# Expert jobs of a DiT block: gathered rows turned by VectorE and dealt out by SyncE instead of turned by TensorE, in eight of sixteen jobs

## The chip, the cores and the metric

The kernel runs on one core of one Trainium2 chip. The metric is the device time of one execution in microseconds, as the median of three runs. The profiler was on for one further execution, and its trace is what all rows below come from. TensorE is called PE, VectorE DVE, ScalarE ACT, GpSimd POOL and SyncE SP, as in the profile.

## The reference, cut to what matters

A transformer block with attention and a mixture of experts, where each expert chooses its tokens. There are 16 x 256 = 4096 tokens of 256 features and 8 experts, so an expert takes 512 tokens.

```python
x = x + o @ Wout.T                            # after attention
tok = x.reshape(-1, d)
gate = jax.nn.softmax(tok @ Wgate.T, axis=-1)
vals, idx = jax.lax.top_k(gate.T, k_cap)      # each expert's 512 tokens
g = _ln(tok[idx_flat], mlp_g, mlp_b).reshape(k_cap, E, d)
y = jnp.einsum('ked,ehd->keh', g, fc1s) + b1s
y = jax.nn.gelu(y, approximate=True)
y = jnp.einsum('keh,edh->ked', y, fc2s) + b2s
y = y * w[..., None]
tok = tok.at[idx_flat].add(y.reshape(-1, d))
```

## The kernel before, in words

Attention comes first, sequence by sequence, in an order written out by hand (the list PLACES). It stores each token's normalised row, without gain and bias, in a DRAM tensor `xn_dram`, and the token itself in the output. The experts follow in 16 jobs of 256 tokens: jobs 0 to 7 are the first halves of the eight experts' lists, jobs 8 to 15 the second halves. Jobs 0 and 1 run inside the ordered plan. For the others there is a loop over `k` from 2 to 15 (L1889) with one iteration a job, and that loop is all that the change touches.

An iteration runs job `k` (`a`) and prepares job `k + 1` (`new`) and job `k + 2` (`far`). It goes through 16 steps `s`, or 15 in iterations 7 to 14 (`seven`). Each engine executes its instructions in the order in which the steps issue them, and SP and POOL issue their DMAs in that order too. What a job needs, with the step before the change:

- `rows` (L1361) for `far`, at step 2, on DVE: which places of the list this job fills. Every second job also needs its pair's counts and sums (`lay_out`, L1874).
- `list_matmul` (L1370) and `take` (L1381) for `new`, at steps 3 and 4 (5 and 6 in iteration 7): PE makes the list in the one PSUM buffer of `pls`, and DVE takes the token numbers into `idx`. `take_gates` (L1392), `gather` (L1398) and `gather_gates` (L1405) come a step later: on POOL two indirect DMAs bring 2 x 128 rows of `xn_dram` into `xg`, and two more the gates into `few`.
- `transposes` (L1414) and `evict` (L1435) for `new`, at step 14 (13 in iterations of 15 steps): PE turns the rows, four 128x128 transposes into `px`, and ACT writes them to `xT` with gain and bias, two activations of 128x256.
- `up` (L1447) and `gelu` (L1455) for job `k`, at steps 0 to 7: one of eight chunks of the hidden layer each.
- Second layer of job `k`, steps 8 to 15. In iterations 2 to 6 and 15 `down` takes a fourth of a half at each step, and `finish` (L1545) writes the weighted rows `y` at steps 11 and 15. In iterations 7 to 14 seven products of half-size blocks take the place of eight (the table SEVEN, L1850): DVE makes sums of weights (`sum_w`, L1477, steps 3 to 6) and of hidden values (`sum_h`, L1486, steps 7 to 10), PE the products (`seventh`, L1495, steps 8 to 14), and DVE adds them up (`mix`, `begin`, `complete`, steps 9 to 14 and step 0 of the next iteration). The first product that reads a sum of hidden values is number 6, at step 9.
- `scatter` (L1551) of job `k - 1` at steps 8 and 12, on POOL: two indirect DMAs that add `y` to the output.
- `far.load()` (L1357) at the end of the iteration, on SP: the 1 MB of w2, the bias row, the 1 MB of w1. They go to the two buffers that the jobs use in turn, so w2 is issued when PE has read job `k`'s w2 for the last time.

In iterations 2 to 6 the second routing runs alongside (`second_routing`, L1865): every fifth step PE counts (`count_three`, L1159, into `pc`), DVE chooses two bits, sets three candidates and compares (`choose_bits` L1163, `compare_three` L1150). The counts fall on steps 4, 9 and 14 of iteration 3, and 3, 8 and 13 of iteration 4. A count reads what the compare before it made.

DVE's transpose turns blocks of 32x32. Attention already uses it with `exchange` (L610): four DMAs on SP, each of which takes 32 partitions apart and lays them out over 128.

Of the kernel before, what the change touches and what calls it, by code (L numbers as in the profile page):

```python
# [9 lines left out]
F32 = mybir.dt.float32  # L10
I32 = mybir.dt.int32
BF16 = mybir.dt.bfloat16
AF = mybir.ActivationFunctionType
# [5 lines left out]
P = 128  # L19
B, N, D = 16, 256, 256  # L20
H, HD = 16, 64
E, DD = 8, 1024
# [5 lines left out]
DC = D // P  # L28
HP = H // 2
FC = DD // P  # L30
KC = CAP // P
KL = KC // 2
CAPL = CAP // 2
SQ = 32
QB = P // SQ
# [3 lines left out]
LN1_G, LN1_B, B_ADA, MLP_G, MLP_B = 0, 2, 4, 6, 8  # L39
# [4 lines left out]
class Plan:  # L44
# [7 lines left out]
    def step(self, place, engine, took, run, needs=(), makes=(), tiles=(), mode=0, lag=0.1):  # L52
        k = len(self.steps)
        self.steps.append((place, engine, took, run, needs, tiles, mode, lag))
        for m in makes:
            self.makers.setdefault(m, []).append(k)
# [7 lines left out]
def kernel(  # L64
# [14 lines left out]
    nc = tc.nc  # L79
# [7 lines left out]
    few = const.tile([P, NVEC + DC * (B + E)], F32, name="few")  # L87
    nc.scalar.dma_start(few, small)
    vec = few[:, :NVEC]
# [133 lines left out]
    PRB = 6  # L223
# [263 lines left out]
    if True:  # L487
        attw = ctx.enter_context(tc.tile_pool(name="attw", bufs=1))
        seq = ctx.enter_context(tc.tile_pool(name="seq", bufs=2))
        work = ctx.enter_context(tc.tile_pool(name="work", bufs=2))  # L490
        stat = ctx.enter_context(tc.tile_pool(name="stat", bufs=4))
        moe = ctx.enter_context(tc.tile_pool(name="moe", bufs=2))
# [114 lines left out]
            engine.tensor_scalar(ws, ws, -1.0 / HD, 1.0, ALU.mult, ALU.mult)  # L607
            engine.tensor_tensor(w3, w3, by_head(ws), ALU.add)

        def exchange(dst, src):  # L610

            for k in (0, 2, 1, 3):
                nc.sync.dma_start(dst[:, k, :], src[k * SQ : (k + 1) * SQ])

        def by_head(x):
            return x.unsqueeze(1).unsqueeze(3).to_broadcast([P, QB, 8, HD // QB])
# [32 lines left out]
        class First:  # L649
# [48 lines left out]
            def evict_too(self, c):  # L698
                b = self.b
                nc.vector.tensor_scalar(  # L700
                    self.out()[:, c, :], self.pt[c], vec[:, LN1_G + c : LN1_G + c + 1],
                    bias1[:, c, b : b + 1], ALU.mult, ALU.add,
                )
# [12 lines left out]
        class Group:  # L716
# [80 lines left out]
            def turn(self, kb):  # L797
                if self.t == 0:
                    kb.append(work.tile([P, QB, TB, HP // 2, SQ], F32, tag="pb", bufs=3, name="kb"))
                nc.vector.transpose(  # L800
                    kb[0][:, :, self.t],
                    self.qk.rearrange("p (q h d) -> p q h d", q=QB, d=SQ),
                )
# [11 lines left out]
            def affine(self):  # L815
                if self.g < 2:
                    qT = of_sequence(qTs, self.b, "qT", [P, HP, N])
                    for t in range(TB):
                        nc.scalar.activation(
                            qT[:, 4 * self.g : 4 * self.g + 4, bass.ts(t, P)].rearrange(  # L820
                                "p h (k m) -> p k h m", m=SQ
                            ),
                            self.raw[:, :, t], AF.Identity, bias=qgb[:, 1:2], scale=qgb[:, 0:1],
                        )
                    return
                kT = self.raw.rearrange("p k t h m -> p (k t h m)")
                nc.scalar.activation(  # L827
                    kT, kT, AF.Identity,
                    bias=vec[:, KN_B : KN_B + 1], scale=vec[:, KN_G : KN_G + 1],
                )  # L830
# [510 lines left out]
        class Job:  # L1341
# [28 lines left out]
            def list_matmul(self):  # L1370
                self.pls = ps.tile([P, KL, P + 2], F32, tag="po", name="pls")
                self.xg = seq.tile([P, KL, D], F32, tag="xs", bufs=5, name="xg")
                self.at = moe.tile([P, KL], F32, tag="at", bufs=4, name="at")
                self.idx = moe.tile([P, 2, KL], I32, tag="idx", bufs=4, name="idx")
                for c in range(KL):
                    nc.tensor.matmul(
                        self.pls[:, c], self.row[:, 1, bass.ts(c, P)], self.pair.ranked,
                        start=True, stop=True,
                    )
# [23 lines left out]
                    )  # L1403

            def gather_gates(self):  # L1405
                self.few = moe.tile([P, KL, E], F32, tag="w", bufs=4, name="few")
                for c in range(KL):
                    nc.gpsimd.indirect_dma_start(
                        out=self.few[:, c, :], out_offset=None, in_=gate_drams[self.tiles][:, :],
                        in_offset=bass.IndirectOffsetOnAxis(ap=self.idx[:, 1, c : c + 1], axis=0),  # L1410
                    )
                self.w = self.few[:, :, self.e]
# [10 lines left out]
            def turned(self):  # L1423
                if self.xT is None:
                    self.xT = seq.tile([P, DC, CAPL], F32, tag="hT", name="xT")
                return self.xT

            def evict_too(self, i):
                c, part = DC - 1, bass.ts(i, P)
                nc.vector.tensor_scalar(  # L1430
                    self.turned()[:, c, part], self.px[c][:, part], vec[:, MLP_G + c : MLP_G + c + 1],
                    vec[:, MLP_B + c : MLP_B + c + 1], ALU.mult, ALU.add,
                )

            def evict(self, chunks=DC, part=slice(0, CAPL)):  # L1435
                for c in range(chunks):
                    nc.scalar.activation(  # L1437
                        self.turned()[:, c, part], self.px[c][:, part], AF.Identity,
                        bias=vec[:, MLP_B + c : MLP_B + c + 1],
                        scale=vec[:, MLP_G + c : MLP_G + c + 1],  # L1440
                    )
                if part.stop == CAPL:
                    self.hid = seq.tile([P, FC, CAPL], F32, tag="qT", name="hid")
                    self.y = work.tile([P, KL, D], F32, tag="pr", bufs=PRB, name="y")
                    self.ph, self.py = {}, {}

            def up(self, f):  # L1447
                self.ph[f] = ps.tile([P, CAPL], F32, tag="sc", bufs=4, name="ph")
# [124 lines left out]
        at = plan.step  # L1573
# [29 lines left out]
        for b in range(B):  # L1603
# [56 lines left out]
            for d in range(HP // 2):  # L1660
                a = Quad(b, d)
                p = base + d * QUAD
# [3 lines left out]
                for i in range(2):  # L1666
                    q = p + 3 * i
                    m = n + (i,)
                    sums, pb, prT = ("sums",) + m, ("pb",) + m, ("prT",) + m
                    scs = [("sc",) + m + (j,) for j in range(2)]  # L1670
                    at(q, "PE", 0.84, partial(a.scores, i), [("qT", b, g), ("kT", b, g)], [("sc",) + m], scs + [("qT", b), ("kT", b)], mode=1, lag=0.22)
                    for j in range(2):
                        nmax, pr, pp = ("nmax",) + m + (j,), ("pr",) + m + (j,), ("sc", 1) + m + (j,)
# [172 lines left out]
        for k in plan.order(PLACES):  # L1846
            plan.steps[k][3]()

        LIST_AT, TURN_AT = 5, 14
        SEVEN = {  # L1850
            3: [("sum_w", 0)], 4: [("sum_w", 1)], 6: [("sum_w", 2), ("sum_w", 3)], 7: [("sum_h", 2)],
            8: [("seventh", 0), ("sum_h", 0)],
# [28 lines left out]
        def listed(job, waits):  # L1881
            yield from ([],) * waits
            yield from ([job.list_matmul], [partial(job.take, c) for c in range(KL)])
            yield [job.take_gates, job.gather, job.gather_gates]
# [4 lines left out]
        for k in range(2, len(jobs)):  # L1889
            a = jobs[k]  # L1890
            new = jobs[k + 1] if k + 1 < len(jobs) else None
            far = jobs[k + 2] if k + 2 < len(jobs) else None
            ahead = k + 1 if k + 1 in FRESH else k + 2
            parts = lay_out(jobs[ahead]) if ahead < len(jobs) and k + 2 not in FRESH else iter(())
            lists = listed(new, 5 if k + 1 in FRESH else 3) if new else iter(())
            more = lay_out(far) if k + 1 in FRESH and far else iter(())
            seven = k in SEVENTHS
            SCATTER_AT = (8, 12) if new else (2, 6)
            if seven:
                a.c = {}  # L1900
            for s in range(15 if seven else 16):
                if k - 1 in SEVENTHS and s == 0:
                    for name, *args in SEVEN[15]:
                        getattr(jobs[k - 1], name)(*args)
                if seven:
                    for name, *args in SEVEN.get(s, ()):
                        getattr(a, name)(*args)
                for step in next(rest, ()):
                    step()
                for step in next(parts, ()):  # L1910
                    step()
                for step in next(lists, ()):
                    step()
                if s > LIST_AT + 4:
                    for step in next(more, ()):
                        step()
                if s in SCATTER_AT:
                    jobs[k - 1].scatter(SCATTER_AT.index(s))
                if new and s == TURN_AT - seven:
                    new.transposes()  # L1920
                    new.evict()
                if s < FC:
                    a.up(s)
                    a.gelu(s)
                    if s == FC - 1:
                        a.weigh()
                elif not seven:
                    i, q = divmod(s - FC, 4)
                    a.down(i, 2 * q, 2 * q + 2)
                    if q == 3:  # L1930
                        a.finish(i)
                        if not new:
                            a.scatter(i)
            if far:
                far.load()
# [54 lines left out]
```

## Time and profile before

| what | us |
|---|---|
| median of 3 runs | 982.57 |
| lowest and highest run | 981.4, 983.54 |
| the profiled execution, its own time | 981.85 |
| its span | 980.1 |
| PE busy | 965.4 |
| DVE busy | 790.2 |
| POOL busy | 654.9 |
| ACT busy | 593.7 |

The span is the time from the first to the last instruction. Busy time counts an engine's own instructions. A line such as L1419 is the line of the kernel that issued an instruction. `out<-in` names tiles. A timeline row gives start, duration, engine, line, operation and count, and in brackets how long the engine had been idle and what ended that. "us to landing" is from the issue of a DMA to its end. The loop begins at about 771 us, and its iterations 3, 4, 9, 10 and 11 begin, with their first `up`, at 786.02, 800.84, 873.59, 887.51 and 901.33.

### The profile page before, as it was taken

What the parts mean: (1) busy time and instruction counts of PE and PEld (TensorE: products, weight loads), DVE (VectorE), ACT (ScalarE), POOL (GpSimd) and SP (SyncE); (2) the same over time, 40 slices, a digit from 0 to 9 for tenths busy, and PEclk for the clock granted to TensorE, in tenths of its full rate; (3) what the DMA queues carried; (4) which work ended last, traced back from release to release, by engine and by line L of the source; (5) the groups of instructions that cost most, each with busy time, mean ns of one, the idle gap of its engine ahead of it and who ended that gap; (6) DMA issues with size and microseconds to landing.
All of it is one profiled execution on the core that took longest, in us unless ns stands there. A gap on an engine that the chain in (4) does not pass through costs nothing.

```text
span 980.1 us, 22623 instructions
## 1 busy us (share of the span) xinstructions
PE 965.4 (99%) x7628; PEld 567.7 (58%) x7628; DVE 790.2 (81%) x1919; ACT 593.7 (61%) x1684; POOL 654.9 (67%) x1069
## 2 busy tenths in 40 slices
PE   9999999999999999999999999999999999999996
PEld 5544544444454545444444544545557888899995
DVE  6678988898899999888899899989975465677661
ACT  2788676667666677667667677666784332343441
POOL 4687677767797886776777677777536435555663
PEclk9999999999999999999999999999999999999998
DMA  8013666666677676667566666777663666776672
GB/s 282 2 43 96 165 176 154 160 168 162 162 189 182 169 173 173 163 174 171 147 175 175 161 168 166 174 178 177 172 189 108 211 183 166 213 200 186 189 221 30
DMA packets 153666, 160.54 MB, mean 164 GB/s; under 512 B 16080, under 2 KB 146640, under 8 KB 153552
## 3 DMA queue, kind: packets, MB, share of 16 engines
q1 hardware_dynamic: 143968, 147.50, 56.5%
q0 software_dynamic: 7168, 8.53, 4.9%
q10 hardware_dynamic: 2416, 3.08, 1.0%
q8 instruction: 61, 1.00, 0.4%
q14 instruction: 53, 0.43, 0.1%
HBM read 53.94 MB, written 12.84 MB: 68 GB/s over the span
## 4 chain that ended last, share of the span: by engine, by line
PE 89%; DMA 3%; issue 2%; DVE 2%; ACT 1%; POOL 1%; SPq 1%; POOLq 0%; DVEq 0%; ACTq 0%
PE pm L519 33%; PE sc L853 12%; PE pw L519 11%; PE po L939 11%; PE ph L1450 10%; PE seven L1506 5%; PE py L1466 4%; DMA out<-y,idx 1%; PE pp L917 1%; PE ph L679 1%; DMA wq<-in_wqkvT 1%; PE px L1419 1%; DMA xg<-xn_dram,idx 1%; ACT pr L875 1%; POOL out L1555 0%
## 5 line engine op out<-in xcount | busy, mean ns | idle before, releaser
L519 PE MATMUL pm<-wq,hT 128*64 128x512 f32 x1536 | 350.0, 595 | 0.2
L886 POOL TENSOR_SCALAR pr<-pr,sums 128x256 f32<-128x256 f32 x512 | 238.1, 485 | 80.7 <-DVE sums L882 59.6
L875 ACT ACTIVATE pr<-sc,nmax 128x256 f32<-128x256 f32 x512 | 237.6, 483 | 65.3 <-DVE nmax L862 54.9
L102 POOL TENSOR_TENSOR ss<-ss,neghalf 128x8 f32<-128x8 f32 x128 | 210.7, 1646 | 10.7
L519 PEld LDWEIGHTS pm<-wq,hT 128*64 128x64 f32 x1536 | 105.5, 137 | 182.8 <-issue 157.5
L862 DVE TENSOR_REDUCE nmax<-sc 128x2 f32<-128x512 f32 x256 | 167.0, 671 | 10.9 <-PE sc L853 10.4
L896 DVE STREAM_TRANSPOSE pb<-pr 128x512 f32<-128x512 f32 x232 | 156.7, 691 | 2.1 <-POOL pr L886 1.3
L744 ACT ACTIVATE sq<-pm 128x512 f32<-128x512 f32 x128 | 77.4, 605 | 105.8 <-PE pm L519 102.6
L853 PE MATMUL sc<-kT,qT 64*64 64x256 f32 x2048 | 126.5, 383 | 0.3 <-ACT kT L827 0.3
L939 PE MATMUL po<-prT,v 128*64 128x256 f32 x1024 | 126.2, 381 | 0.4 <-ACT prT L924 0.3
L519 PE MATMUL pw<-wo,oT 128*64 128x264 f32 x1024 | 126.0, 389 | 0.0
L1450 PE MATMUL ph<-xT,w 128*128 128x256 f32 x512 | 117.2, 383 | 0.3 <-ACT xT L1437 0.3
L748 DVE TENSOR_REDUCE ss<-sq 128x8 f32<-128x512 f32 x128 | 86.0, 672 | 31.3 <-ACT sq L744 30.3
L875 ACT ACTIVATION_READ_ACCUMULATOR pr<-sc,nmax 128x1 f32 x512 | 109.8, 215 | 0.0
L939 PEld LDWEIGHTS po<-prT,v 128*64 128x64 f32 x1024 | 71.4, 137 | 62.9 <-issue 29.8
L853 PEld LDWEIGHTS sc<-kT,qT 64*64 64x64 f32 x2048 | 71.6, 132 | 60.3 <-issue 16.6
L1457 ACT ACTIVATE hid<-ph,few 128x256 f32<-128x256 f32 x128 | 60.1, 474 | 71.6 <-PE ph L1450 67.2
L1450 PEld LDWEIGHTS ph<-xT,w 128*128 128x128 f32 x512 | 94.4, 190 | 13.4 <-ACT xT L1437 1.3
L768 DVE TENSOR_TENSOR qk<-pm,ss 128x512 f32<-128x512 f32 x128 | 89.2, 697 | 11.0 <-POOL ss L102 10.0
L519 PEld LDWEIGHTS pw<-wo,oT 128*64 128x64 f32 x1024 | 70.1, 137 | 42.0 <-issue 8.5
L1400 POOL DMA_INDIRECT xg<-xn_dram,idx x32 | 33.9, 1058 | 84.2 <-DVE idx L1393 42.0
L800 DVE STREAM_TRANSPOSE kb<-qk 128x512 f32<-128x512 f32 x120 | 82.2, 694 | 0.5
(210 smaller groups left out, 1093.4 us busy)
## 6 DMA issues: line engine op xcount, KB each, us to landing
prT<-pb SPq DMA_DIRECT2D x464, 128.0 KB, 2.6
w<-in_fc1T SPq DMA_DIRECT2D x16, 1024.0 KB, 9.6
qraw<-kb SPq DMA_DIRECT2D x120, 128.0 KB, 2.7
kT<-kb SPq DMA_DIRECT2D x120, 128.0 KB, 2.6
w<-in_fc2T SPq DMA_DIRECT2D x15, 1024.0 KB, 6.2
xs<-in_x SPq DMA_DIRECT2D x16, 256.0 KB, 3.2
xT<-in_xT SPq DMA_DIRECT2D x16, 256.0 KB, 3.1
out<-tok SPq DMA_DIRECT2D x32, 128.0 KB, 2.6
```

What stands on the lines that cost most here:

```text
L102: nc.gpsimd.tensor_tensor(dst, src, neghalf[:, : src.shape[1]], ALU.pow)
L519: nc.tensor.matmul(dst[half], weights[:, half], moving, start=start, stop=stop)
L748: nc.vector.tensor_reduce(self.ss[:, 0, :], self.sq.rearrange("p (q e d) -> p e q d", q=QB, e=8), AX.XY, ALU.add,)
L768: engine.tensor_tensor(dst, src.rearrange("p (q e d) -> p q e d", q=QB, e=8), by_head(self.ss[:, 1, :]), ALU.mult,)
L800: nc.vector.transpose(kb[0][:, :, self.t], self.qk.rearrange("p (q h d) -> p q h d", q=QB, d=SQ),)
L853: nc.tensor.matmul(self.sc[i, j][k * HD : (k + 1) * HD, t, :], qTs[self.b][rows, hp, bass.ts(2 * t + k, HD)], keys[rows, hp] if direct els ...
L862: nc.vector.tensor_reduce(self.nmax[i, j], self.sc[i, j], AX.X, ALU.max, negate=True)
L875: nc.scalar.activation(dst, src, AF.Exp, bias=self.nmax[i, j][:, t : t + 1], scale=1.0, accum_out=self.sums[i][:, 0, j, t : t + 1],)
L886: nc.gpsimd.tensor_scalar(self.pr[i, j][:, t, :], self.pr[i, j][:, t, :], self.sums[i][:, 1, j, t : t + 1], 1.0, ALU.mult, ALU.mult,)
L896: nc.vector.transpose(self.pb[i][:, :, :, j].rearrange("p k c t n -> p t k c n"), self.pr[i, j].rearrange("p t (k c m) -> p t k c m", c=TB ...
L939: nc.tensor.matmul(self.po[j * HD : (j + 1) * HD, i, :], vs[self.b][:, c, bass.ts(4 * self.d + 2 * i + j, HD)], prT[:, j, c] if self.whole ...
L1450: nc.tensor.matmul(self.ph[f], self.w1[:, c, bass.ts(f, P)], self.xT[:, c, :], start=(c == 0), stop=(c == DC - 1),)
```

## The change

Eight jobs, 5 to 7 and 11 to 15 (`DEALT`), get another way from `xg` to `xT`. Two DVE transposes (`turn`) write 32x32 blocks of the rows to `blocks`, reading every fourth feature; four DMAs on SP (`deal`) lay them out over 128 partitions in `raw`; two ACT activations (`affine`) apply gain and bias from there to `xT`. The four PE transposes and the two evictions of these jobs go.

Their lists are made one job sooner, for `far` in place of `new`: list at step 5, takes at 6, gathers at 7, and two steps later each (7, 8 and 9) in iterations 3 and 9, where job `k + 1` isn't among the eight and has its own list at steps 3 to 5. `turn` for `far` is at step 13, `deal` at 14, ahead of `far.load()` on SP. `affine` for `new` is at step 12 of the next iteration. In iterations 6 and 14 no list is made. The buffers of `at`, `idx` and `few` go from four to six.

```diff
--- before.py
+++ after.py
@@ -607,10 +607,10 @@
             engine.tensor_scalar(ws, ws, -1.0 / HD, 1.0, ALU.mult, ALU.mult)
             engine.tensor_tensor(w3, w3, by_head(ws), ALU.add)
 
-        def exchange(dst, src):
+        def exchange(dst, src, queue=nc.sync):
 
             for k in (0, 2, 1, 3):
-                nc.sync.dma_start(dst[:, k, :], src[k * SQ : (k + 1) * SQ])
+                queue.dma_start(dst[:, k, :], src[k * SQ : (k + 1) * SQ])
 
         def by_head(x):
             return x.unsqueeze(1).unsqueeze(3).to_broadcast([P, QB, 8, HD // QB])
@@ -1370,8 +1370,8 @@
             def list_matmul(self):
                 self.pls = ps.tile([P, KL, P + 2], F32, tag="po", name="pls")
                 self.xg = seq.tile([P, KL, D], F32, tag="xs", bufs=5, name="xg")
-                self.at = moe.tile([P, KL], F32, tag="at", bufs=4, name="at")
-                self.idx = moe.tile([P, 2, KL], I32, tag="idx", bufs=4, name="idx")
+                self.at = moe.tile([P, KL], F32, tag="at", bufs=6, name="at")
+                self.idx = moe.tile([P, 2, KL], I32, tag="idx", bufs=6, name="idx")
                 for c in range(KL):
                     nc.tensor.matmul(
                         self.pls[:, c], self.row[:, 1, bass.ts(c, P)], self.pair.ranked,
@@ -1403,7 +1403,7 @@
                     )
 
             def gather_gates(self):
-                self.few = moe.tile([P, KL, E], F32, tag="w", bufs=4, name="few")
+                self.few = moe.tile([P, KL, E], F32, tag="w", bufs=6, name="few")
                 for c in range(KL):
                     nc.gpsimd.indirect_dma_start(
                         out=self.few[:, c, :], out_offset=None, in_=gate_drams[self.tiles][:, :],
@@ -1425,6 +1425,36 @@
                     self.xT = seq.tile([P, DC, CAPL], F32, tag="hT", name="xT")
                 return self.xT
 
+            def turn(self):
+                self.blocks = seq.tile([P, QB, DC, KL, SQ], F32, tag="kT", bufs=2, name="blocks")
+                for c in range(KL):
+                    nc.vector.transpose(
+                        self.blocks[:, :, :, c],
+                        self.xg[:, c].rearrange("p (h d q) -> p q h d", q=QB, d=SQ),
+                    )
+
+            def deal(self):
+                self.raw = work.tile([P, QB, DC, KL, SQ], F32, tag="prT", bufs=4, name="dealt")
+                exchange(
+                    self.raw.rearrange("p k h c m -> p k (h c m)"),
+                    self.blocks.rearrange("p q h c m -> p q (h c m)"),
+                )
+
+            def affine(self):
+                for h in range(DC):
+                    nc.scalar.activation(
+                        self.turned()[:, h].rearrange("p (c k m) -> p c k m", k=QB, m=SQ),
+                        self.raw[:, :, h].rearrange("p k c m -> p c k m"), AF.Identity,
+                        bias=vec[:, MLP_B + h : MLP_B + h + 1],
+                        scale=vec[:, MLP_G + h : MLP_G + h + 1],
+                    )
+                self.rooms()
+
+            def rooms(self):
+                self.hid = seq.tile([P, FC, CAPL], F32, tag="qT", name="hid")
+                self.y = work.tile([P, KL, D], F32, tag="pr", bufs=PRB, name="y")
+                self.ph, self.py = {}, {}
+
             def evict_too(self, i):
                 c, part = DC - 1, bass.ts(i, P)
                 nc.vector.tensor_scalar(
@@ -1440,9 +1470,7 @@
                         scale=vec[:, MLP_G + c : MLP_G + c + 1],
                     )
                 if part.stop == CAPL:
-                    self.hid = seq.tile([P, FC, CAPL], F32, tag="qT", name="hid")
-                    self.y = work.tile([P, KL, D], F32, tag="pr", bufs=PRB, name="y")
-                    self.ph, self.py = {}, {}
+                    self.rooms()
 
             def up(self, f):
                 self.ph[f] = ps.tile([P, CAPL], F32, tag="sc", bufs=4, name="ph")
@@ -1846,7 +1874,8 @@
         for k in plan.order(PLACES):
             plan.steps[k][3]()
 
-        LIST_AT, TURN_AT = 5, 14
+        LIST_AT, TURN_AT, DEAL_AT, AFFINE_AT = 5, 14, (13, 14), 12
+        DEALT = (5, 6, 7, 11, 12, 13, 14, 15)
         SEVEN = {
             3: [("sum_w", 0)], 4: [("sum_w", 1)], 6: [("sum_w", 2), ("sum_w", 3)], 7: [("sum_h", 2)],
             8: [("seventh", 0), ("sum_h", 0)],
@@ -1892,7 +1921,8 @@
             far = jobs[k + 2] if k + 2 < len(jobs) else None
             ahead = k + 1 if k + 1 in FRESH else k + 2
             parts = lay_out(jobs[ahead]) if ahead < len(jobs) and k + 2 not in FRESH else iter(())
-            lists = listed(new, 5 if k + 1 in FRESH else 3) if new else iter(())
+            lists = listed(new, 5 if k + 1 in FRESH else 3) if new and k + 1 not in DEALT else iter(())
+            lists_far = listed(far, 5 if k + 1 in DEALT else 7) if k + 2 in DEALT else iter(())
             more = lay_out(far) if k + 1 in FRESH and far else iter(())
             seven = k in SEVENTHS
             SCATTER_AT = (8, 12) if new else (2, 6)
@@ -1911,14 +1941,21 @@
                     step()
                 for step in next(lists, ()):
                     step()
+                for step in next(lists_far, ()):
+                    step()
                 if s > LIST_AT + 4:
                     for step in next(more, ()):
                         step()
                 if s in SCATTER_AT:
                     jobs[k - 1].scatter(SCATTER_AT.index(s))
-                if new and s == TURN_AT - seven:
+                if new and k + 1 in DEALT:
+                    if s == AFFINE_AT:
+                        new.affine()
+                elif new and s == TURN_AT - seven:
                     new.transposes()
                     new.evict()
+                if k + 2 in DEALT and s in DEAL_AT:
+                    (far.turn, far.deal)[DEAL_AT.index(s)]()
                 if s < FC:
                     a.up(s)
                     a.gelu(s)
```

## Rows read from the trace of the kernel before

**Rows 1.** The page: busy time of PE, and the chain that ended last by engine.

```profile
PE 965.4 (99%) x7628; PEld 567.7 (58%) x7628; DVE 790.2 (81%) x1919; ACT 593.7 (61%) x1684; POOL 654.9 (67%) x1069
...
PE 89%; DMA 3%; issue 2%; DVE 2%; ACT 1%; POOL 1%; SPq 1%; POOLq 0%; DVEq 0%; ACTq 0%
```

**Rows 2.** Windows, iterations 4 and 10: us; PE, PEld, DVE, ACT, POOL busy; clock; DMA.

```profile
798.50:813.40 14.90, 14.90 (x78) 12.82 (x76) 10.43 (x65) 4.81 (x10) 8.88 (x9) 1.00 0.66 187
...
900.00:913.80 13.80, 13.80 (x96) 12.77 (x95) 9.49 (x24) 5.88 (x13) 8.49 (x9) 1.00 0.71 201
```

**Rows 3.** Timeline of PE: start, us, line, operation, count.

```profile
813.39 0.27 PE L1419 MATMUL px<-ident,xg 128*128 128x128 f32 x1
...
814.29 1.89 PE L1466 MATMUL py<-w,hid 128*128 128x256 f32 x8
...
900.00 0.60 PE L1419 MATMUL px<-ident,xg 128*128 128x128 f32 x4
900.44 1.06 PE L1506 MATMUL seven<-w,sums 128*128 128x128 f32 x8
...
901.33 2.81 PE L1450 MATMUL ph<-xT,w 128*128 128x256 f32 x12
```

**Rows 4.** The page's costly groups: the transposes on VectorE (count, busy, mean ns).

```profile
L896 DVE STREAM_TRANSPOSE pb<-pr 128x512 f32<-128x512 f32 x232 | 156.7, 691 | 2.1 <-POOL pr L886 1.3
```

**Rows 5.** Line 768 (scale): least, median and greatest ns.

```profile
L768 DVE TENSOR_TENSOR qk<-pm,ss x128: 643/674/1146, 18.1 to 689.3; 128x512 f32<-128x512 f32 x128
```

**Rows 6.** Timeline of SP: an exchange in the middle, two weight loads late.

```profile
303.48 2.49 SPq L613 DMA_DIRECT2D prT<-pb  x4
...
901.53 0.37 SPq L1353 DMA_DIRECT2D w<-in_fc2T  x1
...
902.57 0.42 SPq L1348 DMA_DIRECT2D w<-in_fc1T  x1
```

**Rows 7.** Timeline of POOL, iterations 3 and 9: start, us, operation, idle before.

```profile
794.65 0.98 POOL L1400 DMA_INDIRECT xg<-xn_dram,idx  x1 [0.30 <-DVE enough L1167]
...
798.43 1.62 POOL L1555 DMA_INDIRECT out<-y,idx  x1 [0.30 <-issue]
...
884.69 1.62 POOL L1555 DMA_INDIRECT out<-y,idx  x1 [0.30 <-issue]
...
886.62 1.58 POOL L1555 DMA_INDIRECT out<-y,idx  x1 [0.19 <-issue]
```

**Rows 8.** DMA issues, 794.6 to 795.0: KB and us to landing.

```profile
xg<-xn_dram,idx POOLq DMA_INDIRECT x1, 2.8
```

**Rows 9.** Timeline of DVE, iteration 3: choose_bits to compare_three.

```profile
798.73 0.16 DVE L1167 TENSOR_SCALAR_CACHE_REDUCE enough<-pc 128x3 f32<-128x3 f32 x1 [1.28 <-PE pc L1161]
...
800.71 0.09 DVE L1154 DVE_READ_ACCUMULATOR reach<-gates,three 128x1 bf16 x1
```

**Rows 10.** Timeline of PE: a count in iteration 4, a seventh product in 10.

```profile
803.48 0.17 PE L1161 MATMUL pc<-cnt,twice 128*128 128x3 bf16 x1
...
895.54 1.06 PE L1506 MATMUL seven<-sums 128*128 128x128 f32 x8
```

**Rows 11.** Timeline of DVE, iteration 10: complete, first sum of hidden.

```profile
887.61 0.48 DVE L1528 SCALAR_TENSOR_TENSOR y<-seven,few,y 128x256 f32<-128x256 f32 x1 [1.91 <-PE seven L1506]
...
894.29 0.68 DVE L1493 TENSOR_TENSOR sums<-hid 128x512 f32<-128x512 f32 x1
```

**Rows 12.** DMA issues, 902.5 to 902.9: w1 of job 12.

```profile
w<-in_fc1T SPq DMA_DIRECT2D x1, 1024.0 KB, 10.4
```

**Rows 13.** DMA issues of w1: 768 to 980; 815 to 829; 830 to 844.

```profile
w<-in_fc1T SPq DMA_DIRECT2D x13, 1024.0 KB, 10.0
...
w<-in_fc1T SPq DMA_DIRECT2D x1, 1024.0 KB, 8.4
...
w<-in_fc1T SPq DMA_DIRECT2D x1, 1024.0 KB, 11.7
```

**Rows 14.** DMA issues, 906.5 to 906.9: a gather with w1 in flight.

```profile
xg<-xn_dram,idx POOLq DMA_INDIRECT x1, 6.1
```

## The prediction

> **What bounds it now.** I read the page's busy shares first, then the chain of waits, then one stretch of each kind of iteration, then the order of single instructions. TensorE (PE) is busy 99% of the span and holds 89% of the chain that ended last [rows 1]. In the expert loop it is the whole bound: in iteration 4 it is busy 14.90 of 14.90 us, late in the loop 13.80 of 13.80, where VectorE (DVE) has 9.49, ScalarE 5.88 and GpSimd 8.49 [rows 2]. So an instruction taken from PE is gained in full, and anything that makes PE wait is lost in full. Two facts decide: PE runs in program order, and so do the queues that are to feed it. The averages hide both [rows 2]. The question is what each queue has ahead of the new work at the moment it is wanted.
>
> **What goes.** A job's four PE transposes hold PE from 900.00 to 900.44, so 0.44 us; those of job 5 from 813.39 to 814.29, so 0.90, with a wait for the gather inside [rows 3]. Seven jobs at 0.44 and one at 0.90 give **-3.98 us**. The two evictions of a job on ScalarE become two activations from SBUF, a step or two earlier. ScalarE is idle more than half of either stretch [rows 2], and the data landed an iteration before, so they cost nothing; without that cover PE's first matmul of the next job would wait about 1 us. The six buffers cost nothing that runs.
>
> **What comes, by duration.** Two DVE transposes a job of 128x256. The nearest row is 128x512 at 0.691 [rows 4]; half is 0.35, and I take 0.45 for a fixed part. They read every fourth element; the nearest row for such an order is the tensor_tensor whose median is 674 ns and whose slowest, in the form that writes four apart, 1146 [rows 5], so at worst 0.45 x 1.7 = 0.76. Four DMAs on SP a job: four of the same construction took SP 2.49 to issue [rows 6]. The new ones carry half the bytes in as many pieces; I take 2.49, and 1.5 (four at the 0.37 of a weight load [rows 6]) as the lower end. DVE has room for 0.9 in 13.8, and SP for 2.5. What is not free is where they wait.
>
> [...]
>
> **Cost A, iteration 3.** Job 4 is not dealt, job 5 is. So this iteration makes two lists: GpSimd gets job 4's four indirect DMAs (step 5), a scatter (step 8), job 5's two gathers and two gate gathers (step 9), the second scatter (step 12). DVE is to turn job 5 at step 13. The scatter starts at 798.43, after job 4's four; from it to the next DMA are 1.93 (884.69 to 886.62), and a gather holds the queue 0.98 + 0.30 [rows 7]. So job 5's gathers start at 800.36 and 801.64. The second lands 2.8 later, as one did with no load in flight [rows 8], at 804.44 (none is: SP holds job 5's load behind its deal). DVE ends the turn at 804.9. Behind it on DVE stand choose_bits, candidates and compare_three of the second routing, which ran from 798.73 to 800.80, 2.07 us [rows 9]: now to 806.97. PE's count of them stood at 803.48 [rows 10], a step with nothing to pass it. Loss **3.5 us** (3.4 to 3.8 by the turn's bounds). The next count comes five steps later, so DVE has slack again. Iterations 4 and 5 make one list each, and their gathers cost nothing: up and down matmuls hide them.
>
> **Cost B, iterations 9 and 10.** Job 10 is not dealt, job 11 is: the same double list. GpSimd's first scatter starts at 884.69, so job 11's gathers start at 886.62 and 887.90 [rows 7]; landing 890.70; turn over at 891.15. Behind it on DVE stand job 9's complete, mix and begin, then rows, sums of weights, the list's takes and the first sum of hidden: from the first (887.61) to the last (894.29, 0.68 long) 7.37 us [rows 11]. The new place of the takes, behind the third and fourth weight sum, leaves that total as it is. So the sum is ready at 898.5, and the seventh product that reads it stood at 895.54 [rows 10]. Loss **3.0** (2.8 to 3.4).
>
> **Cost C, jobs 11 to 15.** SP issues in order, and a job's load now stands behind its deal, so behind DVE's turn, so behind the gather. Before, w2's load went out at 901.53, right as PE freed its buffer, and w1's 1.04 later [rows 6], landing 10.4 after that [rows 12]; the median of the 13 is 10.0 [rows 13]. Job 11: 891.15 + 2.49 + 1.04 + 10.0 = 904.7. PE would be there at 901.33 [rows 3] + 3.0 - 0.44 = 903.9: **0.8** lost. Then it goes round: a gather issued while w1 is in flight took 6.1, not 2.8 [rows 14], and came in at about 912.7, when w1 did (902.57 + 10.4 = 913.0 [rows 6, 12]). With the second gather I put 0.4 behind w1. One round is 0.4 + 0.45 + 2.49 + 1.04 + 10.0 = 14.4 against PE's 13.80 - 0.44 = 13.36. Four rounds, jobs 12 to 15: **4.1**. In iterations 4 and 5 the same round of 14.4 just fits PE's 14.90 - 0.44.
> The ends for C are none, if a gather lands 2.8 after its issue, and 9.3, with w1 at 10.9 (14.4 + 0.9 a round, 0.9 more for job 11), part of the way to the slowest 11.7; the quickest was 8.4 [rows 13]. I take the row with a load in flight, since one is in flight at each of these gathers.
>
> **Sum.** -3.98 + 3.5 + 3.0 + 0.8 + 4.1 = +7.4 on the profiled execution's 981.85 (span 980.1 and 1.75 around it), so **989.3**. The median of the runs, 982.57, lies 0.7 above that execution, inside their scatter; I leave it out.
>
> **Rivals.** (1) *The turn is covered*: faster. If the gather is in before DVE reaches step 13, nothing waits, and 981.85 - 3.98 = 977.9. It needs job 5's turn over by 803.48 - 2.07 = 801.4 and job 11's by 895.54 - 7.37 = 888.2. For it: every engine but PE has time to spare [rows 2]. Against it: GpSimd's own order puts the second gather's start at 801.6 and 887.9. (2) *A and B without C*: the gathers share the DMA engines with w1 and land early, the loads stay on time, and it is 981.85 - 3.98 + 3.5 + 3.0 = 984.4. For it: job 5's gathers in the quiet; against it: 6.1 [rows 14]. (3) *Only one of the double lists bites*, because PE has other work to run on: 981.85 - 3.98 + 3.5 = 981.4, no change.
> [...]
>
> **Chances.** A measurement here tells 0.2%, 2 us, from no change: 980.6 to 984.5 is the same. Forecast 0.62, own range 985 to 994. Rival 1 0.16. Rival 2 0.15, half of it on either side of 984.5. Rival 3 0.07. So slower 0.62 + 0.08 = 0.70, same 0.07 + 0.07 = 0.14, faster 0.16. The range takes in rivals 2 and 3 and the forecast with C's upper end: 980 to 994; rival 1 and a little above stay out.
>
> **What would show it.** Right: in iteration 4 a gap on PE of some 3.5 before a count (pc) that VectorE ends, and in iteration 10 one before a seventh product; DVE's turns idle for "DMA xg" at jobs 5 and 11; w2's loads issued 3 us and more into the next iteration, and PE waiting for w1. Wrong: turns that start at once after begin, loads at the iteration's end as before, PE without gaps, and the span shorter by 4. C alone is wrong if PE waits twice and then runs at 13.4 an iteration.

## The result, and the profile after

The changed kernel takes **995.23 us** (median of six runs, 993.19 to 998.55) against 982.22 in six runs of the kernel before: a ratio of 1.013, interval 1.0118 to 1.0143. So it is slower, as forecast, but by 13 us and not 7; 995.2 lies above the range of 980 to 994. The profiled execution took 996.0, its span is 994.3.

The page of the changed kernel: the busy times, and the chain that ended last by engine, the lines that answer to [rows 1].

```profile
PE 966.5 (97%) x7595; PEld 565.7 (57%) x7596; DVE 798.6 (80%) x1935; ACT 593.4 (60%) x1684; POOL 652.4 (66%) x1069
...
PE 8%; DMA 6%; DVE 2%; issue 2%; POOL 1%; SPq 0%; POOLq 0%; ACT 0%; DVEq 0%
```

The second line adds up to about a fifth of the span, so the chain was followed back through the end of the execution only, and its 8% can't be set against the 89% of before. In that part transfers have 6 against PE's 8. PE's busy sum did not fall by the 4 us of transposes that went, it rose by 1.1. Some 2.7 of this difference is a way of counting (0.17 at each of 16 waits, below), and 1.7 are matmuls that became slower; the windows below show which.

The waits of PE from 771 to 985 us of the kernel before: a single one.

```profile
PE px L1419 <- DMA xg<-xn_dram,idx: 0.2, 1, 0.2
```

The same view of the changed kernel, without its last and smallest line (us in total, times, longest):

```profile
PE ph L1478 <- DMA w<-in_fc1T: 6.8, 6, 2.5
PE pc L1161 <- DVE reach L1154: 2.6, 1, 2.6
PE ph L1478 <- DVE y L1556: 1.0, 1, 1.0
PE pls L1376 <- DVE row L1366: 0.8, 3, 0.3
PE pls L1376 <- DVE idx L1393: 0.5, 1, 0.5
PE seven L1534 <- DVE sums L1521: 0.5, 2, 0.2
PE seven L1534 <- DVE idx L1393: 0.3, 1, 0.3
```

The three costs of the prediction stand here in their order of size: the wait for w1 is C, the count (`pc`) that waits for the compare is A, and B is in the lines with `y` L1556, `row` and `sums` (of the last two, one wait each is in iteration 10). Each wait costs about 0.17 more than its row says: a `seven` of eight matmuls starts at 903.22 and lasts 1.06, and the next, without a wait, starts 0.89 after it, at 904.11. So the row of such matmuls ends 0.17 after the next can begin, and idle time counted from there is that much short.

The timeline of the changed kernel holds all three (start, us, engine, what it does, and idle time before it with what ended that). The first five lines of the fence are iterations 3 and 4, the next six iteration 10, the rest iterations 11 to 15.

```profile
800.75 0.99 POOL L1400 DMA_INDIRECT xg<-xn_dram,idx  x1 [0.30 <-issue]
802.04 0.96 POOL L1400 DMA_INDIRECT xg<-xn_dram,idx  x1 [0.30 <-issue]
...
803.51 0.64 DVE L1431 STREAM_TRANSPOSE blocks<-xg 128x256 f32<-128x256 f32 x1 [4.85 <-DMA xg<-xn_dram,idx]
804.81 0.63 DVE L1431 STREAM_TRANSPOSE blocks<-xg 128x256 f32<-128x256 f32 x1 [0.66 <-DMA xg<-xn_dram,idx]
...
807.44 0.16 PE L1161 MATMUL pc<-cnt,twice 128*128 128x3 bf16 x1 [2.59 <-DVE reach L1154]
...
894.34 0.64 DVE L1431 STREAM_TRANSPOSE blocks<-xg 128x256 f32<-128x256 f32 x1 [0.60 <-DMA xg<-xn_dram,idx]
...
895.01 2.49 SPq L613 DMA_DIRECT2D dealt<-blocks  x4
...
896.74 1.10 PE L1478 MATMUL ph<-xT,w 128*128 128x256 f32 x4 [1.00 <-DVE y L1556]
...
897.60 0.56 SPq L1353 DMA_DIRECT2D w<-in_fc2T  x1
...
898.92 0.42 SPq L1348 DMA_DIRECT2D w<-in_fc1T  x1
...
902.22 1.16 PE L1534 MATMUL seven<-sums 128*128 128x128 f32 x8 [0.23 <-DVE sums L1521]
...
909.05 4.55 PE L1478 MATMUL ph<-xT,w 128*128 128x256 f32 x20 [1.21 <-DMA w<-in_fc1T]
...
909.56 1.16 DVE L1431 STREAM_TRANSPOSE blocks<-xg 128x256 f32<-128x256 f32 x2 [3.15 <-DMA xg<-xn_dram,idx]
...
910.75 2.49 SPq L613 DMA_DIRECT2D dealt<-blocks  x4
...
969.22 8.83 PE L1478 MATMUL ph<-xT,w 128*128 128x256 f32 x32 [2.50 <-DMA w<-in_fc1T]
```

Read the fence as one chain per job: gather (POOL), turn (DVE), deal, w2, w1 (SP), up phase (PE). Before, SP's weight loads [rows 6] stood apart from the first three links; the count answers to the one of [rows 10], which had no wait.

Where the time came, from the first `up` of each iteration, changed kernel against the one before:

| stretch | before | after | difference |
|---|---|---|---|
| iteration 3 | 14.82 | 15.63 | +0.8 |
| iteration 4 | 15.18 | 18.43 | +3.2 |
| iterations 5 to 8 | 57.57 | 56.98 | -0.6 |
| iterations 9 and 10 | 27.74 | 31.60 | +3.9 |
| iterations 11 to 14 | 55.39 | 60.17 | +4.8 |
| job 15 to the end | 23.38 | 25.08 | +1.7 |

With 0.4 ahead of iteration 3 this is the 14.2 between the spans. The last line has no counterpart in the prediction. It is in the windows (start:end, length, PE busy, PEld, DVE, ACT, POOL, granted clock, DMA, GB/s):

```profile
972.00:973.00 1.00, 1.00 (x4) 0.82 (x3) 0.00 (x0) 0.24 (x1) 0.81 (x3) 0.50 0.48 32
...
974.00:975.00 1.00, 1.00 (x6) 0.89 (x5) 0.00 (x0) 0.36 (x1) 0.00 (x0) 1.00 0.62 51
```

After PE's wait of 2.50 the granted clock was 0.50 from about 970.5 to 974, and the 32 matmuls of job 15's up phase took 8.67 (969.22 to 977.89).

### The profile page after: what moved, and what is told of

The parts are those of the page before. It is cut to its first block, busy times and chain, and to the rows that moved or that the text cites. A ratio compares the mean times of both kernels' runs of the same rounds, so it can differ in the third digit from the quotient of the medians.

```text
span 994.3 us, 22629 instructions
## 1 busy us (share of the span) xinstructions
PE 966.5 (97%) x7595; PEld 565.7 (57%) x7596; DVE 798.6 (80%) x1935; ACT 593.4 (60%) x1684; POOL 652.4 (66%) x1069
## 5 line engine op out<-in xcount | busy, mean ns | idle before, releaser
L1485 ACT ACTIVATE hid<-ph,few 128x256 f32<-128x256 f32 x128 | 60.2, 474 | 119.5 <-PE ph L1478 110.5
L1478 PE MATMUL ph<-xT,w 128*128 128x256 f32 x512 | 119.8, 387 | 8.4 <-DMA w<-in_fc1T 6.8
```

Source lines behind the costliest of these rows:

```text
L1478: nc.tensor.matmul(self.ph[f], self.w1[:, c, bass.ts(f, P)], self.xT[:, c, :], start=(c == 0), stop=(c == DC - 1),)
```

## The experiments

The theories: **S**, the order on SP makes C (weights behind the deal, behind the turn, behind the gather); **T**, the deal's bytes compete with the loads; **D**, DVE's added work is what PE waits for. A and B are put down to the double lists of iterations 3 and 9. The kernel before ran beside each.

**The deal left out.**

```diff
@@ deal
-                self.raw = work.tile(...)
-                exchange(...)
+                pass
@@ affine
-                        self.raw[:, :, h].rearrange("p k c m -> p c k m"), AF.Identity,
+                        self.blocks[:, :, h].rearrange("p k c m -> p c k m"), AF.Identity,
```

> The deal is left out: the activations read the turned blocks where they lie, so the rows are not laid out over the partitions and the eight jobs compute on wrongly placed features. Everything else of the change stays: the lists a job sooner, the turns on VectorE, their place. Theory S (SyncE's order: a job's weights stand behind its deal, that behind the turn, that behind the gather) expects the waits for w1 to go, 6.8 us in the changed kernel's profile, and the fall of the clock in the last job, 1.7: 986.7 us, between 985 and 988.5. Theory D (VectorE's added work is the cost) expects 993 or more. Theory T (the deal's traffic slows the loads) expects the same as S here.

Measured: 992.22, ratio 1.0109 (1.0092 to 1.0126). No wait for w1 is left and iterations 11 to 14 take 13.2 to 13.4 each, 53.3 together, so C is gone, as S has it. But the total, outside the 985 to 988.5 of S, fell by 3 and not by 8, for iteration 4 became 7.2 longer than before instead of 3.2. Its timeline (SP, DVE, PE):

```profile
803.16 0.42 SPq L1348 DMA_DIRECT2D w<-in_fc1T  x1
...
807.79 0.63 DVE L1431 STREAM_TRANSPOSE blocks<-xg 128x256 f32<-128x256 f32 x1 [3.63 <-DMA xg<-xn_dram,idx]
...
810.42 0.17 PE L1161 MATMUL pc<-cnt,twice 128*128 128x3 bf16 x1 [5.58 <-DVE reach L1154]
810.82 3.78 PE L1474 MATMUL ph<-xT,w 128*128 128x256 f32 x8 [0.23 <-DVE y L1570]
```

With no deal ahead of it, job 5's load goes out at once (w2 at 802.12, w1 at 803.16) and is in flight with the second gather, which lands 5.7 after its issue at 802.03 instead of 2.7. The turn is 3.0 later than in the changed kernel (807.79 against 804.81), and the count with it. In the changed kernel the load held behind the deal had shielded the gather. On top of that the granted clock was 0.50 from 808 to 814 and eight `up` matmuls took 3.78 (1.99 in the changed kernel). The first 2.5 us of this lay in the wait and cost nothing: with waits of 6.15 and 0.90 of transposes gone, about 2 us of the 7.2 are left for the clock.

**The deal with 1/32 of the bytes:** the same four DMAs, at the same place in SP's order, of one source partition each.

```diff
@@ deal
-                exchange(...)
+                for k in (0, 2, 1, 3):
+                    nc.sync.dma_start(dst[:QB, k, :], src[k * SQ : k * SQ + 1])
```

> Four DMAs still wait for the turn and still stand ahead of the weights on SyncE, but each moves one source partition of 32, so a 32nd of the bytes; the activations read the blocks where they lie (the rest of the dealing is left out). Theory S expects nearly the time of the changed kernel, 992 to 996 us, as the wait and the 2.5 us of issue stay. Theory T expects the loads back on time, about 987.

Measured: 992.62, ratio 1.011 (1.0089 to 1.013). SP's timeline and PE's wait for w1:

```profile
897.25 2.45 SPq L1441 DMA_DIRECT2D dealt<-blocks  x4
899.80 0.39 SPq L1353 DMA_DIRECT2D w<-in_fc2T  x1
...
900.87 0.43 SPq L1348 DMA_DIRECT2D w<-in_fc1T  x1
```

```profile
PE ph L1478 <- DMA w<-in_fc1T: 2.7, 3, 1.2
```

The total is where S expected it, but the timeline divides C between S and T. The waits for w1 fell from 6.8 to 2.7, and iterations 11 to 14, from the first line below to the second, take 56.5: between the 60.2 of the changed kernel and the 53.3 without a deal. So in these four rounds 3.7 us go with the bytes and 3.2 stay without them.

```profile
911.28 4.55 PE L1478 MATMUL ph<-xT,w 128*128 128x256 f32 x20 [1.20 <-DMA w<-in_fc1T]
...
967.79 7.15 PE L1478 MATMUL ph<-xT,w 128*128 128x256 f32 x32
```

Of the 3.7, 1.4 lie between w1's landing and the deal, 1.4 between w1's issue and the next up phase, and 0.8 between w2's issue and w1's: with the full deal in flight SP takes 1.32 for that (897.60 to 898.92), here 1.07. The four issues cost about the same, 2.45 to 2.80 here and 2.49 to 2.74 with all the bytes. The total hides this, for here the clock fell behind the count (eight `up` matmuls took 3.61, in the changed kernel 1.99), and this profiled execution began iteration 3 1.6 later.

**w2 ahead of the deal, w1 behind it.**

```diff
@@ end of the iteration (and the deal's call at DEAL_AT[1] taken out)
-                far.load()
+                far.load_down()
+                if k + 2 in DEALT:
+                    far.deal()
+                far.load_up()
```

> The whole change, with one order turned: at the end of an iteration SyncE issues w2 and the bias row of a job, then its deal, then w1. Theory S expects w2 to start as before the change, its 6 us to cover the deal, and w1 nearly on time: most of the 6.8 + 1.7 comes back, 986.5 to 989 us. What is left is the double lists in iterations 3 and 9. Theory T expects no more than 2 us of gain, since the same bytes still go ahead of w1; theory D expects none.

Measured: 992.77, ratio 1.0111 (1.009 to 1.0132), about 4 above the upper end that S gave. PE's waits:

```profile
PE pc L1161 <- DVE reach L1154: 5.7, 1, 5.7
```

No wait for w1 in any job: with w2 first C is gone, the deal and its bytes still being there, so it is the order that lets both parts of C reach PE. But A has grown as in the first experiment, for the same reason (w2 goes out at 802.16, ahead of job 5's second gather being in, which landed 5.9 after its issue), and the clock was at 0.50 behind it. PE's wait for `y` L1556, the largest of B, grew from 1.0 to 1.9. Two effects of opposite sign hide in one total; only the timeline parts them.

**The first job behind a double list turned one iteration later.**

```diff
+        LATE, LATE_AT = (5, 11), (5, 6)
@@
+                if k + 1 in LATE and s in LATE_AT:
+                    (new.turn, new.deal)[LATE_AT.index(s)]()
-                if k + 2 in DEALT and s in DEAL_AT:
+                if k + 2 in DEALT and k + 2 not in LATE and s in DEAL_AT:
```

> The whole change, but jobs 5 and 11, whose lists share iterations 3 and 9 with another, are turned and dealt in the next iteration (steps 5 and 6) in place of steps 13 and 14. If the double list made VectorE wait as costs A and B say, TensorE's wait for the count in iteration 4 goes (3.6 with the wait for y behind it) and that in iteration 10 (about 3, less about 1 that the turn at step 5 now takes from the weight sums), while the round of jobs 12 to 15 stays: 988 to 990.5 us. If the lists were innocent, 994 to 996.

Measured: 988.25, ratio 1.0058 (1.0041 to 1.0075), as expected. PE's waits:

```profile
PE ph L1478 <- DMA w<-in_fc1T: 4.6, 4, 2.6
...
PE seven L1534 <- DVE sums L1521: 0.5, 1, 0.5
```

The count's wait and the one for `y` are gone: A and B came from DVE waiting for the gather of a double list with the routing's compare and the sevenths behind it. C stays.

**Both edits together,** the whole change with w2 first and jobs 5 and 11 late:

```diff
+                if k + 2 in DEALT and k + 2 not in LATE and s == DEAL_AT[0]:
+                    far.turn()
@@
+                far.load_down()
+                if k + 2 in DEALT and k + 2 not in LATE:
+                    far.deal()
+                far.load_up()
```

> The whole change with both cures: w2 ahead of the deal on SyncE, and jobs 5 and 11 turned in the next iteration. All sixteen turns on VectorE, all deals and all lists stay. Theory S expects no wait for w1, none for the count, so that TensorE's 3.98 us come through, less the wait for the one list buffer in iteration 3 (0.5) and some 0.7 where job 11's takes and turn hold up sums of hidden values: 979 us beside 981.6 for the kernel before, between 978 and 980.5. If VectorE's turns or the deal's traffic cost time of their own, it stays above 982.

Measured: **980.62** (11 runs), against 982.05 (23 runs of before): ratio 0.9986, interval 0.9977 to 0.9995. This is a little above the 978 to 980.5 that S gave, and faster than the kernel before by 1.4 us: little, but with an interval that leaves out 1. The page and all of PE's waits in the loop:

```profile
PE 962.1 (98%) x7596; PEld 564.7 (58%) x7596; DVE 799.0 (82%) x1935; ACT 593.6 (61%) x1684; POOL 650.4 (66%) x1069
```

```profile
PE pls L1376 <- DVE idx L1393: 0.5, 1, 0.5
PE seven L1534 <- DVE sums L1521: 0.3, 1, 0.3
PE seven L1534 <- DVE idx L1393: 0.2, 1, 0.2
PE pls L1376 <- DVE row L1366: 0.2, 1, 0.2
```

DVE does all 16 transposes of the eight turns here (799.0 busy, as in the changed kernel) and SP all eight deals, and yet it is faster than before: D falls, and so does T as a cause that acts without the order. Of the 3.98 of transposes, 1.2 of waits and 0.17 for each of the four go back: 2.1 left by this sum, 1.7 between the spans (980.1 and 978.4).

**The same with the dealt lists later** (step 8 in iteration 3, 9 in iteration 9), to take away the wait for `idx`.

```diff
-            lists_far = listed(far, 5 if k + 1 in DEALT else 7) if k + 2 in DEALT else iter(())
+            lists_far = listed(far, 5 if k + 1 in DEALT else 8 if k < 8 else 9) if k + 2 in DEALT else iter(())
```

> As with both cures, and the second list of iteration 3 starts at step 8 instead of 7, that of iteration 9 at step 9. The list buffer is then free when TensorE comes, and job 11's takes stand behind the last sum of hidden values. Expected 0.5 to 0.8 us less than with both cures alone, 978.3 us; if the lists' places are of no account, the same time.

Measured: 980.88, ratio 0.9987 (0.9977 to 0.9996): no difference. The wait for `idx` went, and another came:

```profile
PE pc L1161 <- DVE reach L1154: 0.8, 1, 0.8
```

**Does the wait make the clock fall?** Three kernels put transposes of the identity that no one reads into a wait. The first, on the kernel without the deal:

```diff
+                if (k, s) == (4, 3):
+                    fill(48)
```

> The kernel without the deal again (it computes on wrongly placed features), with 48 transposes of the identity into a spare bank put ahead of the count in iteration 4, some 5.2 us of TensorE work that nothing reads, in the place of its wait of 5.6. If the wait let the clock fall, as the records of that kernel show (half speed from 807.9 for 6.8 us, so 3.4 lost), the clock stays up and the time comes to 988.8 us from 992.2. If the 3.4 have another cause, it stays at 992 or gets worse.

Measured: 997.98, ratio 1.0165 (1.015 to 1.018). It tells nothing of a filled wait, for the filler itself waited for its PSUM buffer until the original wait was over. A later wait of the same execution, in iteration 10, matters below: the four matmuls behind it took 1.10, as four do in the changed kernel behind the wait of 1.00.

```profile
PE fill L508 <- DVE y L1570: 6.4, 1, 6.4
```

```profile
907.49 1.10 PE L1474 MATMUL ph<-xT,w 128*128 128x256 f32 x4 [2.84 <-DVE y L1552]
```

The second repeats it in other buffers (`mm`).

> The kernel without the deal (the features it computes on are wrongly placed), with 48 transposes of the identity ahead of the count of iteration 4, in a PSUM buffer that is free at that time, so that they run inside the wait of 5.6 us instead of behind it. 48 at 0.11 are 5.3 us. If the idle time made the clock fall: clock 1.00 behind it and 3.4 us less than without the fill, about 988.8. If not: clock 0.5 for 6.8 us as before, 992.2.

Measured: 995.95, ratio 1.014 (1.0123 to 1.0157). Still too late: 3.94 of the wait had passed before the filler began, here behind DVE's read of the last count, and the clock had fallen by then. In iteration 10 a wait of 2.40 was followed by a clock of 0.50 (timeline, then windows):

```profile
808.81 8.16 PE L513 MATMUL fill<-ident 128*128 128x128 f32 x48 [3.94 <-DVE enough L1172]
...
906.04 1.55 PE L1479 MATMUL ph<-xT,w 128*128 128x256 f32 x4 [2.40 <-DVE y L1557]
```

```profile
806.00:808.00 2.00, 0.00 (x0) 0.00 (x0) 0.00 (x0) 0.00 (x0) 1.42 (x1) 0.89 1.03 298
808.00:810.00 2.00, 1.19 (x6) 1.20 (x7) 1.82 (x11) 0.00 (x0) 0.00 (x0) 0.50 0.97 326
```

It is no test of filling the wait, and lengthened the iteration by its own work. Both expectations also put the clock's price at 3.4, half of the 6.8; as the first experiment shows, about 2 could have been gained.

The third fills job 15's wait in the changed kernel.

```diff
+                if (k, s) == (len(jobs) - 1, 0):
+                    fill_mm(20)
```

> The changed kernel with one thing more: 20 transposes of the identity, which no one reads, before the first up matmul of job 15, where TensorE waited 2.5 us for w1 and its granted clock was then half for 3.4 us. At 0.11 us each they take 2.2 us, so they lie inside the wait. If the idle time is what made the clock fall: granted clock 1.00 all through job 15's up phase, that phase 7.0 instead of 8.7 us, and a total of about 993.5. If the clock falls for another reason: clock again 0.5 there, and 995.2, no difference.

Measured: 996.63, ratio 1.0142 (1.0125 to 1.0159), in total no gain on the changed kernel's 995.23. The timeline, then the window of the up phase and two behind the count of iteration 4:

```profile
808.52 0.16 PE L1166 MATMUL pc<-cnt,twice 128*128 128x3 bf16 x1 [2.62 <-DVE reach L1159]
808.92 3.43 PE L1483 MATMUL ph<-xT,w 128*128 128x256 f32 x8 [0.23 <-DVE y L1579]
...
970.40 2.35 PE L513 MATMUL fill<-ident 128*128 128x128 f32 x20
972.59 7.07 PE L1483 MATMUL ph<-xT,w 128*128 128x256 f32 x32
```

```profile
810.00:812.00 2.00, 2.00 (x7) 1.61 (x6) 1.90 (x13) 0.47 (x1) 0.00 (x0) 0.54 0.80 141
812.00:814.00 2.00, 2.00 (x12) 1.70 (x11) 1.80 (x11) 0.95 (x2) 0.22 (x1) 1.00 1.03 335
...
974.00:976.00 2.00, 2.00 (x11) 1.77 (x10) 0.00 (x0) 1.07 (x3) 1.81 (x3) 1.00 0.30 21
```

The local forecast held: with the wait filled the clock stayed at 1.00 and the up phase took 6.90 (972.59 to 979.49) instead of 8.67. The total's forecast of 993.5 did not. In the profiled execution the clock also fell behind two earlier waits, 2.62 ahead of the count and 2.79 for w1 of job 11, where the changed kernel's profiled execution kept it (behind 2.59 and 1.21), and iteration 3 began 1 us later. For the other three runs of this kernel there is no trace to say the same.

## Why the prediction was right and wrong

**The step that failed.** The sum was 6.8 short. The prediction let each wait of PE cost its own length and left the clock out without a reason, which was 1.7 in job 15; and it took one round of C at 14.4 where 15.04 was measured, above all because two turns and not one follow w1's landing. C came to 7.9 (4.8 of the table, 4 x 0.44 of transposes and 1.4 ahead of job 11) against its 4.9, and inside its bounds of none to 9.3; the clock and small losses outside the three costs took the time past the range.

**Right: the direction and the three places.** Inside its iteration the count was 2.76 later than before (5.40 after the first `up`, 807.44 - 802.04, against 2.64), and with the 0.8 by which iteration 3 already ran late that is 3.6 for **A's** 3.5. The compare ended at 807.39; with the 0.39 taken off by which iteration 3 began late that is 807.00, and the prediction said 806.97. DVE's turn for job 11 ended at 894.98; less the 3.86 by which iteration 9 began late it is 891.12, and the prediction's step said 891.15. The product that reads the first hidden sum was 6.7 later than before (902.22 - 895.54), of which 3.86 are from ahead of iteration 9: 2.8 for **B's** 3.0. Iteration 9 had 0.7 of it and iteration 10 2.1, in three waits rather than one; the largest, 1.00, came earlier, at an `up` waiting for the DVE work of job 9 (`y` L1556). The sum itself was ready at 902.17, which is 898.31 with the 3.86 taken off; the prediction said 898.5. That A and the waits of iteration 10 come from the gathers of a double list is shown by the run that turns jobs 5 and 11 later.

**C: the right mechanism, the wrong size.** The four rounds took 60.17 instead of 4 x 14.4. By the prediction's own terms, summed over the four:

| term | predicted | measured |
|---|---|---|
| from w1's landing to the deal (gather 0.4 and turn 0.45) | 3.4 | 5.7 |
| deal's start to w2's issue | 10.0 | 10.6 |
| w2's issue to w1's | 4.2 | 5.1 |
| w1's landing | 40.0 | 38.8 |

The first term failed most. With w2 and w1 in flight both gathers come in almost together (8.2 and 7.1 after their issue at 901.37 and 902.66), so two turns follow w1 and not one: 1.16. A turn took 0.635 at the median, inside the bounds of 0.35 to 0.76 but not the 0.45 taken. The third term had been read from SP without a deal in flight. By the tiny deal, the deal's bytes are in the first, third and fourth term (1.4, 0.8 and 1.4).

**Steps that failed elsewhere.** "In iterations 4 and 5 the same round of 14.4 just fits" did not hold for job 5, whose load went out behind A's late turn: PE waited 0.75 for its w1, 0.9 with the overlap. Nor did it fit by its own terms: 14.90 is the length of a window, while iteration 4 takes 15.18 before, 14.28 without job 5's 0.90. "Iterations 4 and 5 make one list each, and their gathers cost nothing" was said of the gathers and left out the list matmuls before them: three waited for DVE's `row` (0.8 in all), one of them in iteration 5, which so gained nothing; and the second list of iterations 3 and 9 waits until DVE has read the first out of the one PSUM buffer (`idx`, 0.5 and 0.3). The two waits for `idx` added nothing to the total here: PE came to the late count, and to the late sum, that much later and waited less. They show with both edits, where A and B are gone.

**Missing: the clock.** The last wait cost 1.7 more than its length, at half the clock: job 15 has no gain to give back, and 1.7 is what the table shows there. Table against terms, the missing 6.8 is 1.7 for the clock, 2.4 for C's rounds, 1.5 in iterations 3 and 4, 0.3 in 5 and 6, 0.5 in 9 and 10 and 0.4 ahead of iteration 3.

**Rivals.** The covered turn (1) is excluded by the 4.85 that DVE sat idle for job 5's gather. Rival 3 is excluded by both places losing. Rival 2, A and B without C, is excluded by the 6.8 of waits for w1. The gather did not pass along with a load: 2.7 in the quiet, 5.7 (first experiment) and 8.2 with w2 and w1 in flight. With loads in flight it took two to three times as long, so they give it no cover.

## What to carry to other kernels

Before work is moved to an idle engine, ask what stands behind it in that engine's order and in the DMA queue's: here two DVE instructions of 0.64 cost 3.2 in one iteration, because a routing step was queued behind them while they waited for a gather, and four weight loads in turn came late for the same reason on SP. Put a transfer whose buffer is free ahead of one that has to wait, and start the consumer of a late gather a stage later; with both, the same instructions were 1.4 us faster than before instead of 13 slower. And look at the timeline of each run, not at its total: twice a removed wait was given back by a load that had been held off a gather.

## What the hardware showed that was not expected

- In the loop, in the profiled executions of the changed kernel and the experiments, PE waited 2.4 to 2.9 us eight times. Six of these waits were followed by a granted clock of 0.50 for about 3.4 us, which cost 1.7: 2.40 (second filled kernel), 2.50 (changed kernel), 2.58 (tiny deal), 2.61 (late turns), 2.62 and 2.79 (last wait filled). Two were not: 2.59 in the changed kernel and 2.84 in the first filled one. In four longer waits, ahead of the count of iteration 4 (5.58, 5.74, 6.37, and 3.94 ahead of a filler), the clock fell inside the wait and stayed at 0.50 for about 6.8 us; of that only the part behind the wait costs, about 2 us in the kernel without the deal. After waits of 1.9 and less the rows show 1.00, and up to the last matmul the clock fell nowhere in the loop without one of these longer waits. That the idle time brings it about fits all of this, and the filled wait of job 15; but two waits that were not filled kept 1.00 as well, so that one trace does not prove it, and which waits are spared stays open.
- Four small DMAs took SP 2.49 to 2.74 to issue with 64 KB each and 2.45 to 2.80 with 1/32 of that: between these two sizes the issue went by the DMA and not by the byte. Right behind w2, as in the kernel with both edits, it took up to 3.52.
- Loads of 1 MB that follow such a deal on SP are issued more slowly: up to 0.56 for w2 against 0.38 to 0.39 behind the tiny deal.
